# A graph network on one core: the sums of messages by destination are narrowed to 80 nodes, and the node stage's groups are put between them

## The chip, the cores and the metric

The kernel runs on one core of a Trainium2 chip. The metric is the device time of one execution in microseconds; the kernel before has a median of 4238.74 us over three runs (4227.38 to 4244.78). Engines are named as in the profile: PE is the matrix engine, PEld its loading of weights, DVE the vector engine, ACT the scalar engine, POOL the general engine (it also issues the indirect DMAs), SP the engine that only issues DMAs.

## What is computed

Two graph layers over 6250 nodes of 128 features and 100000 edges, each followed by a residual and a normalisation over the features. The edges come sorted by `dst`. The first layer is attention: a score for each edge and head, a softmax over the edges of one `src`, then the weighted values summed by `dst`. The second computes a message for each edge from both of its nodes and sums it by `src`.

```python
edge_index = jnp.stack([src, dst])
x = _layernorm(x + _L0_gnn_ref(x, edge_index, edge_attr_8, ...))
# first layer, cut:
weighted = v[src] * weights[:, :, None]
out = jax.ops.segment_sum(weighted, dest, num_segments=N).reshape(N, F)
return out @ Wo.T + bo
# second layer, cut:
edge_in = jnp.concatenate([x[row], x[col], edge_features], axis=-1)
h = jax.nn.silu(edge_in @ eW1 + eb1)
agg = jax.ops.segment_sum(jax.nn.silu(h @ eW2 + eb2), row, num_segments=N)
return jax.nn.silu(jnp.concatenate([x, agg], axis=-1) @ nW1 + nb1) @ nW2 + nb2
```

In the inputs, `dst` is the integer part of 6250 times the square of a uniform number. So edge number k of the sorted list has a `dst` near 6250 (k/100000)^2, and low nodes have many more edges than high ones.

## The kernel before

Edges are handled in tiles of 128, 784 tiles in all; 16 tiles are a chunk (49 chunks), 4 tiles a quad (196 quads). The first 9 chunks (region 0) go to the lowest nodes and are summed elsewhere, over the first 256 nodes. The rest, chunks 9 to 48, is region 1: 40 chunks, 160 quads. Nodes are handled in 49 blocks of 128.

The stages follow each other. A sort by `src` writes each edge's record to its place (up to line 898). The first layer's messages are computed in the order of `src` and scattered back to a table `xmsg` in the order of `dst` (L1008 and before). While the sort runs, `rows_of_keys` (L269) prepares what the later sums need: `d0q`, the first `dst` of each quad, and `dq`, each edge's `dst` less that of its quad. It also fills `bad`, a table of flags. If a flag is set (the keys don't have the form that the fast arm needs), `xflag` is 0 and a general arm runs in place of `fast()`. One of them (L322) is set where a `dst` lies 128 or more above its quad's first.

**Sums by dst** (L1090 to L1112). For each chunk one DMA loads its messages, `mt`, 1 MB, in turn from SP's and ACT's queue, with four buffers. For each quad DVE writes `ohd` (L1105), four one-hot matrices of 128 edges by 128 nodes, in one instruction of 512 elements a partition. PE multiplies (L1110): the messages of a tile are the stationary operand (128x128, f32), the one-hot matrix moves, and four products add up in one PSUM tile `ps` (six buffers). DVE adds `ps` to `agg` at the column of the quad's first node, which is read from a register (L1112). `agg` holds features by nodes.

**Node stage** (L1115 to L1170). The 49 blocks form 13 groups of four (the last has one). A group goes through three functions:

- `residual`: four products with `wo` into `po` (L1124), the bias added to `x_sb` by POOL (L1126; this depends on no sum, and all thirteen run early), `x_sb` plus `po` on DVE (L1127), and mean and variance per node on DVE (L902, L903).
- `normal`: the square root on ACT (L906), its reciprocal on DVE (L907), the normalisation in place, one DVE instruction per block (L1139), a transpose on PE (L1141) into `xp`, and a copy to `x1t` on ACT (L1142).
- `parts_of`: the products with `wab` into `pa` (L1151), halves copied by ACT (L1153) and added to `b1` by DVE (L1154), a store to `b_tab` from SP (L1156), a split of the other half into three bf16 parts by ACT and POOL in turn (L1161 to L1164), and a store to `a3_tab` (L1165; the profile names it a_tab).

```python
for g in range(len(groups) + 2):
    for lag, step in enumerate((residual, normal, parts_of)):
        if 0 <= g - lag < len(groups):
            step(g - lag)
```

**Edge stage** (from L1175). POOL gathers rows of `b_tab` (L118), SP loads one-hot rows (L1184), edge features (L1200) and windows of `a3_tab` (L1204), and PE works through 196 steps of four tiles.

Each engine takes its instructions in order. The order on an engine is not the one of the program's text: a scheduler in the framework places instructions by its own estimate of times, keeps dependencies, and adds the semaphores. Pools close at the end of a `with`, and their memory passes to the next.

## Time and profile before

| | us |
|---|---|
| three runs, median (lowest to highest) | 4238.74 (4227.38 to 4244.78) |
| the profiled execution | 4211.11 |
| its span | 4209.2 |
| from the last step before the sums to the last sum, about | 2954 to 3116 |
| node stage to the first gather of the edge stage | 3116 to 3174 |
| edge stage to the end | 3174 to 4209 |

Busy shares over the whole span: PE 63%, DVE 47%, ACT 20%, POOL 51%. The profile's page is one execution with every instruction's start and duration. Two kinds of answers are used besides the page. A timeline lists start, duration, engine, line, operation and tiles, with "x" and a number where equal instructions are merged. A table of windows gives, for a stretch, the busy time of each engine, the granted clock of PE as a share of full speed, and the DMA engines' share. An f32 product shows as two records on PE. Where a matmul's record overlaps the next one, the cost is read from start to start and not from its duration.

### The profile page before, as it was taken

Reading aid. Unit: us, or ns where it says so; the run is one execution under the profiler, and the core shown is the slowest. Engines: PE = TensorE matmul, PEld = TensorE weight load, DVE = VectorE, ACT = ScalarE, POOL = GpSimd, SP = SyncE. Lnnn points to the kernel's source line nnn. Section 1 sums busy time; section 2 is a strip of 40 time slices with the busy share of each in tenths; the row PEclk is TensorE's granted clock in tenths of the full one; section 3 lists DMA queues with packets and bytes.
Section 4 is the critical chain, followed back from the end, with each engine's and each line's share of the span. In section 5 each row is a group of like instructions: output and inputs, shape, how many; then the busy total and the mean of one; then the engine's idle time right before and its main releaser. Section 6 shows DMA issues by size and latency. Waiting matters only on the chain. (4 is left out here: it accounts for less than half of the span.)

```text
span 4209.2 us, 65902 instructions
## 1 busy us (share of the span) xinstructions
PE 2643.5 (63%) x22552; PEld 2030.1 (48%) x22552; DVE 1994.6 (47%) x6056; ACT 861.8 (20%) x2688; POOL 2156.6 (51%) x2119
## 2 busy tenths in 40 slices
PE   6546674444444225555655666565895999898988
PEld 4444443333333224444544555454883666665655
DVE  6655335454545525555555556554892222222232
ACT  2222232122222111111111111110022222222222
POOL 3455544555555551445445444556216666666663
PEclk8555555566555556666676777576897899999999
DMA  5433545444543315434434344431754333333341
GB/s 180 130 118 103 143 138 168 139 151 132 167 130 100 110 60 142 135 109 133 122 113 127 114 120 117 138 98 50 281 197 128 109 100 98 99 110 98 101 124 46
DMA packets 492378, 523.75 MB, mean 124 GB/s; under 512 B 155562, under 2 KB 417117, under 8 KB 486912
## 3 DMA queue, kind: packets, MB, share of 16 engines
q1 hardware_dynamic: 399150, 345.09, 28.3%
q0 software_dynamic: 66048, 140.62, 10.9%
q10 hardware_dynamic: 26834, 33.73, 2.5%
q8 instruction: 180, 2.95, 0.3%
q14 instruction: 166, 1.36, 0.1%
HBM read 391.11 MB, written 128.06 MB: 123 GB/s over the span
## 5 line engine op out<-in xcount | busy, mean ns | idle before, releaser
L126 POOL DMA_INDIRECT xs<-stg,posi x784 | 803.9, 1025 | 766.1 <-ACT cs L777 337.0
L126 POOL DMA_INDIRECT xmsg<-msg,at x640 | 648.7, 1014 | 722.1 <-issue 409.4
L118 POOL DMA_INDIRECT bt<-b_tab,dsti x640 | 640.5, 1001 | 333.4 <-issue 165.4
L778 PE MATMUL base<-hi,lo 128*128 128x49 bf16 x784 | 169.6, 216 | 547.3 <-ACT cs L777 333.5
L780 PEld LDWEIGHTS <-hit 128*128 128x128 bf16 x2352 | 145.7, 116 | 546.5 <-issue 531.0
L1259 DVE TENSOR_TENSOR stat_r<-stat_r,ps 128x128 f32 x232 | 66.3, 286 | 645.7 <-PE ps L1255 223.4
L787 PE MATMUL kx<-kw,ohd 128*128 128x128 bf16 x2352 | 265.5, 284 | 97.0 <-issue 56.9
L762 DVE TENSOR_SCALAR_CACHE_REDUCE junk<-sk,meta 128x127 bf16<-128x127 int16 x784 | 298.1, 435 | 11.4 <-DMA sk<-skew 4.8
L777 ACT CAST cs<-base 128x49 bf16<-128x49 f32 x784 | 160.7, 205 | 638.3 <-remote 286.4
L787 PEld LDWEIGHTS <-ohd 128*128 128x128 bf16 x2352 | 213.9, 131 | 136.1 <-issue 129.3
L587 PEld LDWEIGHTS <-oht 128*128 128x128 bf16 x2352 | 219.3, 134 | 124.3 <-issue 63.8
L1255 PE MATMUL ps<-ohf,fe 128*128 128x128 f32 x1568 | 231.4, 292 | 52.1 <-issue 28.5
L587 PE MATMUL qv<-qw,oht 128*128 128x128 bf16 x1920 | 200.5, 287 | 97.7 <-DVE oht L576 36.3
L1240 PE MATMUL po<-w_sb,ht 128*128 128x128 f32 x1568 | 245.6, 301 | 18.7 <-issue 9.4
L1255 PEld LDWEIGHTS ps<-ohf,fe 128*128 128x128 f32 x1568 | 208.8, 205 | 62.0 <-issue 33.9
L1240 PEld LDWEIGHTS po<-w_sb,ht 128*128 128x128 f32 x1568 | 205.2, 203 | 66.8 <-issue 49.4
L979 PE MATMUL qv<-vw,oht 128*128 128x128 bf16 x1920 | 188.5, 257 | 74.2 <-DVE pr L590 34.0
L1232 ACT ACTIVATE ht<-pre 128x512 f32<-128x512 f32 x196 | 116.9, 597 | 493.1 <-PE pre L1228 199.6
L979 PEld LDWEIGHTS <-oht 128*128 128x128 bf16 x1920 | 152.9, 117 | 122.6 <-issue 92.3
L223 DVE TENSOR_TENSOR lo<-iota_e,lo_c 128x2048 bf16<-128x2048 bf16 x98 | 119.0, 1215 | 150.6 <-remote 80.2
L780 PE MATMUL look<-st_b,hit 128*128 128x49 bf16 x1568 | 164.3, 211 | 27.1 <-DVE sel L794 17.0
L1228 PE MATMUL pre<-oht,aw 128*128 128x512 bf16 (+1 forms) x696 | 171.9, 365 | 12.8 <-issue 12.4
(303 smaller groups left out, 5228.8 us busy)
## 6 DMA issues: line engine op xcount, KB each, us to landing
st<-xs SPq DMA_DIRECT2D x49, 1128.0 KB
srow<-slo_row SPq DMA_DIRECT2D x98, 512.0 KB
lob<-lob_row SPq DMA_DIRECT2D x49, 512.0 KB
drow<-dlo_row SPq DMA_DIRECT2D x49, 512.0 KB
sk<-skew SPq DMA_DIRECT2D x49, 508.0 KB
qw<-q_tab SPq DMA_DIRECT2D x232, 96.0 KB
vw<-v_tab SPq DMA_DIRECT2D x232, 96.0 KB
aw<-a_tab SPq DMA_DIRECT2D x232, 96.0 KB
```

Of the source, the lines that this page charges most:

```text
L118: nc.gpsimd.indirect_dma_start(out=dst, out_offset=None, in_=table, in_offset=bass.IndirectOffsetOnAxis(ap=idx, axis=0))
L126: apart(nc.gpsimd.indirect_dma_start(out=table, out_offset=bass.IndirectOffsetOnAxis(ap=idx, axis=0), in_=src, in_offset=None), group)
L587: nc.tensor.matmul(qe[:, i, :], w["oh"][:, 4 * q + i, :], w["qw"][:, (4 * q + i) // WT[r], k, :], start=(k == 0), stop=(k == 2))
L762: nc.vector.tensor_scalar(junk, w["sk"][:, :, j], meta[:, c * UC + j, 0:1], 0.0, ALU.is_equal, ALU.add, accum_out=w["rank"][:, j:j + 1])
L777: nc.scalar.copy(cs, base)
L778: nc.tensor.matmul(base, lo, hi, start=False, stop=False, skip_group_check=True)
L780: nc.tensor.matmul(w["look"][:, j - 8 * h, :], w["hit"][:, j, :], tab, start=(i == 0), stop=(i == 2))
L787: nc.tensor.matmul(kx[:, i, :], w["ohd"][:, 4 * q + i, :], w["kw"][:, q, a, :], start=(a == 0), stop=(a == 2))
L979: nc.tensor.matmul(ve[:, i, :], w["oh"][:, 4 * q + i, :], w["vw"][:, (4 * q + i) // WT[r], k, :], start=(k == 0), stop=(k == 2))
L1228: nc.tensor.matmul(pre[:, i * wt:(i + 1) * wt, :], w["aw"][:, 4 // wt * q + i, k, :], w["oh"][:, 4 * q + i * wt:4 * q + (i + 1) * wt, :], ...
L1240: nc.tensor.matmul(po[:, i, :], ht[:, i, :], cw["w2"], start=False, stop=(i == 3))
L1255: nc.tensor.matmul(ps[:, i // WT[r], :], fe_[:, i, :], oh[:, i, :], start=(i % WT[r] == 0), stop=((i + 1) % WT[r] == 0))
```

## The change

There are four edits. The sums by `dst` use one-hot matrices, products and adds of 80 nodes (`WD`) instead of 128, and the flag is set at 80 in region 1. A second flag says that a quad's first `dst` must not lie over 64 nodes under the curve 0.16384 q^2 (q is the quad's number). By that curve `ready[g]` tells after which quad no later sum can reach the group g: 60, 82, 99, 114, 127, 139, 150, 160, 169, 178 and 187 for groups 0 to 10, of quads 36 to 195. The steps of these eleven groups are written between the quads, one step after a quad; groups 11 and 12 follow at the end, step by step. And the normalisation is done by ACT, as scale and bias of an ACTIVATE, with the bias `off`, minus mean times `rstd`, from DVE. `mt` gets five buffers instead of four, `ps` four instead of six, `po` and `xp` one instead of two; the zeroing of `agg2` and the load of `x_sb` are written one chunk earlier.

```diff
+WD = 80
+DST_SQ = 0.16384
+DST_SLACK = 64.0
...
-        nc.vector.tensor_single_scalar(b[:p, 1:2], b[:p, 1:2], float(P), ALU.is_ge)
+        nc.vector.tensor_single_scalar(b[:p, 1:2], b[:p, 1:2], float(WD if r else P), ALU.is_ge)
...
+            early = ks.tile([1, nt // 4], F32, name="early")
+            nc.gpsimd.iota(early, pattern=[[1, nt // 4]], base=t0 // 4, channel_multiplier=0,
+                           allow_small_or_imprecise_dtypes=True)
+            nc.vector.scalar_tensor_tensor(early, early, DST_SQ, early, ALU.mult, ALU.mult)
+            nc.vector.tensor_sub(early, early, d0qf)
+            nc.vector.tensor_reduce(b[0:1, 2:3], early, AX.X, ALU.max)
+            nc.vector.tensor_single_scalar(b[0:1, 2:3], b[0:1, 2:3], DST_SLACK, ALU.is_gt)
...
-        with tc.tile_pool(name="n0", bufs=3) as np_, tc.tile_pool(name="n0q", bufs=2, space=PSUM) as npq:
+        ready = [min(NQ, int((((j0 + n) * P + DST_SLACK) / DST_SQ) ** 0.5) + 1) for j0, n in groups]
+        with tc.tile_pool(name="fd", bufs=2) as dp, tc.tile_pool(name="fdp", bufs=4, space=PSUM) as dpp, \
+             tc.tile_pool(name="n0", bufs=3) as np_, tc.tile_pool(name="n0q", bufs=2, space=PSUM) as npq:
...
-                po = npq.tile([P, 4, F], F32, name="po")
+                po = npq.tile([P, 4, F], F32, name="po", bufs=1)
...
-                xp = npq.tile([P, 4, P], F32, name="xp")
+                off = np_.tile([P, 4, 1], F32, name="off")
+                nc.vector.scalar_tensor_tensor(off[:, :n], mv[:, :n, 0:1], -1.0, rstd[:, :n], ALU.mult, ALU.mult)
+                xp = npq.tile([P, 4, P], F32, name="xp", bufs=1)
                 for i in range(n):
-                    nc.vector.tensor_scalar(x_sb[:, j0 + i, :], x_sb[:, j0 + i, :], mv[:, i, 0:1], rstd[:, i, :],
-                                            ALU.subtract, ALU.mult)
+                    nc.scalar.activation(x_sb[:, j0 + i, :], x_sb[:, j0 + i, :], AF.Identity, bias=off[:, i, :],
+                                         scale=rstd[:, i, :])
...
+            def by_group():
+                for g in range(len(groups) - 2):
+                    for step in (residual, normal, parts_of):
+                        yield ready[g]
+                        step(g)
+                for step in (residual, normal, parts_of):
+                    for g in range(len(groups) - 2, len(groups)):
+                        yield NQ
+                        step(g)
+                yield NQ + 1
...
+            for c in range(AC, NC):
...
+                mt = dp.tile([P, UC, F], F32, name="mt", bufs=5)
...
+                if c == AC + 3:
+                    nc.gpsimd.memset(agg2, 0.0)
+                    nc.scalar.dma_start(x_sb, x_n)
+                for q in range(4):
+                    oh = dp.tile([P, 4, WD], F32, name="ohd", bufs=4)
...
+                    ps = dpp.tile([F, WD], F32, name="ps")
+                    for i in range(4):
+                        nc.tensor.matmul(ps, mt[:, 4 * q + i, :], oh[:, i, :], start=(i == 0), stop=(i == 3))
+                    to = agg[:, bass.ds(bs[4 * c + q - b0], WD)]
+                    nc.vector.tensor_add(to, to, ps)
+
+                    if due <= 4 * c + q + 1:
+                        due = next(node_steps)
+            while due <= NQ:
+                due = next(node_steps)
```

More of the change, by code (lines that the diff above doesn't have):

```diff
@@ L1089, in fast @@
         nc.scalar.copy(agg[:, :AB * P], nearby)
-        with tc.tile_pool(name="fd", bufs=2) as dp, tc.tile_pool(name="fdp", bufs=6, space=PSUM) as dpp:
-            pairs = xmsg.rearrange("(p t) f -> p t f", p=P)
-            for c in range(AC, NC):
-                if c == AC or c % 4 == 0:
-                    bs = regs(d0q, 4 * c, 4 * (4 - c % 4), ENG.DVE, NP - 1)
-                    b0 = 4 * c
-                mt = dp.tile([P, UC, F], F32, name="mt", bufs=4)
-                cuts = (0, 4, 8, 16) if c == AC else (0, 16)
-                for t0, t1 in zip(cuts, cuts[1:]):
-                    (nc.sync if c % 2 else nc.scalar).dma_start(mt[:, t0:t1], pairs[:, c * UC + t0:c * UC + t1, :])
-                if c == AC + 4:
-                    nc.gpsimd.memset(agg2, 0.0)
-                    nc.scalar.dma_start(x_sb, x_n)
-                for q in range(4):
-                    oh = dp.tile([P, 4, P], F32, name="ohd", bufs=4)
-                    nc.vector.tensor_tensor(
-                        oh, iota_f[:, None, :].to_broadcast([P, 4, P]),
-                        dq[:, c * UC + 4 * q:c * UC + 4 * q + 4, None].to_broadcast([P, 4, P]), ALU.is_equal)
-                    ps = dpp.tile([F, P], F32, name="ps")
-                    for i in range(4):
-                        nc.tensor.matmul(ps, mt[:, 4 * q + i, :], oh[:, i, :], start=(i == 0), stop=(i == 3))
-                    to = agg[:, bass.ds(bs[4 * c + q - b0], P)]
-                    nc.vector.tensor_add(to, to, ps)
         groups = [(j0, min(4, NB - j0)) for j0 in range(0, NB, 4)]
-        with tc.tile_pool(name="n0", bufs=3) as np_, tc.tile_pool(name="n0q", bufs=2, space=PSUM) as npq:
+        ready = [min(NQ, int((((j0 + n) * P + DST_SLACK) / DST_SQ) ** 0.5) + 1) for j0, n in groups]
+        with tc.tile_pool(name="fd", bufs=2) as dp, tc.tile_pool(name="fdp", bufs=4, space=PSUM) as dpp, \
+             tc.tile_pool(name="n0", bufs=3) as np_, tc.tile_pool(name="n0q", bufs=2, space=PSUM) as npq:
             held = {}
@@ L1165, in parts_of @@
                 nc.sync.dma_start(rows_of(a3_tab, j0, n), a3[:, :n].rearrange("p j i f -> p j (i f)"))
-            for g in range(len(groups) + 2):
-                for lag, step in enumerate((residual, normal, parts_of)):
-                    if 0 <= g - lag < len(groups):
-                        step(g - lag)
+            def by_group():
[8 more added lines that the diff above has]
+                yield NQ + 1
+            node_steps = by_group()
+            due = next(node_steps)
+            pairs = xmsg.rearrange("(p t) f -> p t f", p=P)
+            for c in range(AC, NC):
+                if c == AC or c % 4 == 0:
+                    bs = regs(d0q, 4 * c, 4 * (4 - c % 4), ENG.DVE, NP - 1)
+                    b0 = 4 * c
+                mt = dp.tile([P, UC, F], F32, name="mt", bufs=5)
+                cuts = (0, 4, 8, 16) if c == AC else (0, 16)
+                for t0, t1 in zip(cuts, cuts[1:]):
+                    (nc.sync if c % 2 else nc.scalar).dma_start(mt[:, t0:t1], pairs[:, c * UC + t0:c * UC + t1, :])
+                if c == AC + 3:
[3 more added lines that the diff above has]
+                    oh = dp.tile([P, 4, WD], F32, name="ohd", bufs=4)
+                    nc.vector.tensor_tensor(
+                        oh, iota_f[:, None, :WD].to_broadcast([P, 4, WD]),
+                        dq[:, c * UC + 4 * q:c * UC + 4 * q + 4, None].to_broadcast([P, 4, WD]), ALU.is_equal)
+                    ps = dpp.tile([F, WD], F32, name="ps")
[6 more added lines that the diff above has]
+            while due <= NQ:
+                due = next(node_steps)
         byd.close()
```

## The prediction

> **What bounds the kernel now.** The diff touches one stretch of the span, so I read it first in a table of three windows: the sums by dst, the node stage, the first 58 us of the edge stage. Columns: length, then busy us of PE, PE's weight loads, DVE, ACT, POOL, then granted clock, DMA share, GB/s.

> ```profile
> 2984.00:3116.00 132.00, 131.51 (x1176) 131.39 (x1176) 125.97 (x296) 0.00 (x0) 0.75 (x1) 1.00 0.79 270
> 3116.00:3174.00 58.00, 43.87 (x247) 35.14 (x246) 52.46 (x206) 33.72 (x79) 28.00 (x24) 0.99 0.41 131
> 3174.00:3232.00 58.00, 23.78 (x73) 12.33 (x73) 7.58 (x13) 4.70 (x8) 40.70 (x43) 0.56 0.43 125
> ```

> In the sums PE is never idle, DVE nearly never, ACT and POOL always. In the node stage DVE is busiest and PE still works 44 of 58 us. Next the timeline in the sums, to see who sets the pace:

> ```profile
> 3105.39 0.29 DVE L1112 TENSOR_TENSOR agg<-agg,ps 128x128 f32 x1
> 3105.59 0.68 DVE L1105 TENSOR_TENSOR ohd<-iota_f,dq 128x512 f32<-128x512 f32 x1
> 3106.28 0.29 DVE L1112 TENSOR_TENSOR agg<-agg,ps 128x128 f32 x1
> ```

> One quad per 0.89 us (3105.39 to 3106.28). The chain of waits has 131.60 us of PE ps L1110 x1176 in one piece: 0.1119 us a record, eight records a quad (four products, each two records), 0.895. Where DVE catches up (timeline, 2990.17 to 2990.97) a quad takes it 0.80. So **PE sets the pace, DVE is 10% behind it**.

> The node stage, from the chain (start, us, what):

> ```profile
> 3136.70 1.17 POOL res L1162
> 3137.89 0.63 ACT a L1163
> 3138.58 1.16 POOL a L1164
> 3139.74 0.69 issue
> 3140.47 1.17 POOL res L1162
> ```

> A period of 3.77 us per group: two POOL subtractions with casts on ACT between them. How it hands over, from SyncE's timeline:

> ```profile
> 3170.84 0.50 SPq L1156 DMA_DIRECT2D b_tab<-ab  x1
> 3173.80 7.41 SPq L1165 DMA_DIRECT2D a_tab<-a  x2
> 3182.64 0.34 SPq L1184 DMA_DIRECT2D srow<-slo_row  x1
> ```

> The last sum is added at 3116.40. b_tab's last store is issued at 3170.84 and POOL's first gather starts at 3174.06 (57.7 after the sum). The last a_tab store waits behind POOL's gathers, and SP reaches the edge stage's loads at 3182.64 (66.2 after). From there to 3232 PE waits for rows that SP loads.

> **Step 1, 80 columns instead of 128.** DVE: ohd is 0.683 us at 512 elements and the 256-element tensor_tensor of L113 0.411, so 1.06 ns an element; 192 fewer save 0.20, and 48 fewer in the add 0.05. DVE's quad goes from 0.80 to 0.55. PE is what counts: the moving side shrinks, the stationary side (mt, 128x128 f32, loaded anew for every record) doesn't. The trace has no f32 product at 80 columns. Low end: only columns count, 0.1119 x 80/128 = 0.070. High end: none do, 0.112. The nearest row is an f32 product with as large a stationary and 49 columns, at granted clock 0.50 (table of windows, 313 to 315), beside the sums' own product, also at 0.50 (2966 to 2968):

> ```profile
> 313.36 0.64 PE L356 MATMUL ps<-cnt,ones_f 128*128 128x49 f32 x2
> 313.80 0.63 PE L357 MATMUL ps<-cnt,after 128*128 128x49 f32 x2
> ```

> ```profile
> 2965.98 2.05 PE L1110 MATMUL ps<-ohd,mt 128*128 128x128 f32 x8 [6.91 <-DMA mt<-xmsg]
> ```

> Two records of 49 columns take 0.44 us from pair to pair, 0.22 each. The eight of 128: 2.05 less the last one's 0.55 is 1.50 over seven gaps, 0.214. So 49 columns cost as much as 128: **the weight load is the floor**, and at 128 columns the stream has just reached it. I take 0.1119 at 80 columns: step 1 gives PE nothing, and frees DVE.

> [...]

> **Step 2, eleven groups between the quads.** Per group of four blocks PE gets 8 records of po (0.112), 4 transposes (0.11) and 8 of pa with 256 columns (0.216; each from start to start of its line's records in the node stage, L1124, L1141, L1151): 0.90+0.44+1.73 = 3.06 us; eleven groups 33.7. PE is full, so all of it lengthens the sums. DVE per group: add 0.60, statistics 4x0.26, reciprocal and off 0.25, two adds of b1 0.66, together 2.6; 160x0.55 + 11x2.6 = 117 us, well under PE, so even POOL's hold on it is covered (with POOL's bias adds running before 2984, ohd took 1.55 instead of 0.68). ACT had 0.75 us there: free. DMA moved 270 GB/s at share 0.79 and 420 in 2966 to 2968; eleven groups' stores of 640 KB fit.

> New waits, by the changed kernel's order of instructions:
> - po reads agg, and the next dynamic add must wait for po. The order puts po 1.5 to 3 quads behind the add that it needs, so PE hardly waits for it; then the adds stand behind x_sb's add and the statistics on DVE, with four ps buffers now instead of six: about 0.3 us a group.
> - The transposes come 3.25 to 9.5 quads (2.9 to 8.5 us) after po. Their chain on DVE and ACT: 1.22 from po to the add (as at 3116.54 to 3117.76), add 0.60, sums and statistics 1.5, sqrt with its wait 0.5, reciprocal and off behind quads' work 1.0, first normalisation 0.6: 5.4. Groups 7 and 8 with 3.25 and 4 quads wait 1.7 and 1, four others 0.5, and a spacing of 0.40 on ACT against 0.2 to 0.45 on PE costs 0.2 a group: 7 us.
> - pa waits for x1t (0.58 and two handovers) behind 1.25 quads: 0.1 to 0.2 a group.

> Sum **11 us** (4 if every chain is hidden by the quads, 20 if ACT's and DVE's queues double it). mt's issues on ACT sit in front of square roots and copies, but each waits for a quad that PE passes before the transposes in question, so they cost nothing; with five buffers a load has 14 us.

> **Step 3, normalisation on ACT.** Four ACTIVATEs instead of four DVE instructions of 0.400. The nearest row with one pointer is L605 (0.405 at 129 elements); one without, L606, is 0.310. A second pointer: 0 to 0.1. ACT is free in the sums, so only the tail pays. What hides it otherwise is ACT's idleness; without that, 11x1.6 us.

> **Start.** x_sb still loads first, the first data still come at 2966. While POOL adds the bias (to 2984.7) ohd sets a pace of 1.68; five quads of that gain 0 to 3 us with the smaller ohd: 1.5.

> **The check** adds five DVE instructions and one POOL iota on 160 elements some 2.7 ms earlier: under 1 us, beside the sort's matmuls.

> **Step 4, the tail.** Only groups 11 and 12 (five blocks) follow. In us after PE's last work of the sums, each step by its row in the node stage of before (po as at 3116.54 to 3117.76, casts 0.62, POOL 1.16 and 0.43, ab 0.37): po and add 1.8, statistics 2.9, sqrt, reciprocal, off 3.7, five normalisations 5.9, transpose and x1t 7.2, ten records of pa 9.4, ab and b1's add 10.2, cast 10.9, res of both, cast, a of both 14.7. First gather at 15.2 (57.7 before), SP's loads at 16.5 (66.2 before, since POOL now ends a before it gathers). So 42.5 us by POOL, 49.7 by SP. I take SP's: PE's gaps from 3190 on end with what SP loads.

> **Sum.** The end of the sums moves by 33.7+11-1.5 = +43.2, from 3116.4 to 3159.6; the handover gives back 49.7: -6.5, or +0.7 by POOL. I take **-6**: 4211.1 (the profiled execution; its span is 4209.2) becomes 4205. The median of the runs shown, 4238.74, lies 0.66% above that execution, so the forecast for the median is **4233**. No change of under 0.5% (21 us) can be told from none here. PE's own work bounds the gain as well: with no stall at all the sums would end at 3148.6, 11 us earlier than I take, so step 1 as I price it allows 18 us at most.

> **Rivals.**
> 1. *Records shrink with the columns* (0.070). Quads then cost PE 0.57; DVE binds: 147x0.55 + 11x2.6 + 9 us of waits for po + 8 of POOL's hold from 2983 gives 3111, and the gain is 66.2-16.5+5 = 55: 4184. For it: bf16 products of 49 columns just beside L356 (L780, 314.23 to 314.46) come 0.04 apart, so few columns can be fast. Against: those in f32 aren't, and an f32 product's weight load shows 0.191 (L1151, L1124) where an f32 transpose's shows 0.141 (L1141). 13%, half-way records included.
> 2. *The node steps hold the quads* (slower). PE takes its instructions in order; if a transpose or pa not yet ready stops the quads behind it for more than the order planned, the stall is per group. With four ps buffers it can reach 3.5 to 4 us (5.4 of chain less what is queued ahead): 41 instead of 11, net +24: 4262. It decides from 3.5 us a group. Against: the order's 4 to 9 quads of distance, which at 0.89 last longer than at any faster pace. 15%.
> 3. *The wide arm isn't taken*: if a quad spanned 80 nodes the flag would choose the general arm. The reference's dst, sorted, spans at most 65 in a quad, and lies at most 21.3 nodes under the curve of the check, which allows 64. 1%, several hundred us slower, no estimate from this trace.

> **Numbers.** Forecast 71% (4233; by its own bounds, 4 to 20 us of stalls and 42 to 50 of handover, 4220 to 4250, and the runs' own spread of 17 us on top). Rival 1 13%, rival 2 15%, rival 3 1%. Range 4196 to 4263: it leaves out most of rival 1 and the far end of 2. Faster by over 0.5% (under 4217.5): rival 1 and a tenth of the forecast, 0.20. Slower (over 4260): two thirds of rival 2, rival 3 and some of the forecast, 0.15. Same 0.65.

> **What would show it.** Right: ps records with 80 columns still 0.11 apart at full clock; quads' stretches without groups 0.89 each; DVE with gaps in the sums; sums' end near 3160, first gather some 15 us later, SP's first edge load near 3176. Wrong: records near 0.07; PE idle over 2 us at every group; an edge stage that starts earlier than SP's loads allow or later than both.

## The result and the profile after

The changed kernel takes 4267.23 us (median of 8 runs, 4260.26 to 4285.08), the kernel before 4236.59 in the same comparison (8 runs, 4221.04 to 4245.91): **1.0085 times, 95% interval 1.0061 to 1.0109**, 31 us slower. The forecast was 4233, and 4267 lies above its range.

The profiled executions (4267.90 after, 4211.11 before) are 57 us apart, because the one of before was 25 us below its median. So I compare the stretch that the change touches. It is counted from the first record of DVE's one-hot line (a wait, at 2954.05 before and 2979.05 after; the first one-hot itself starts 0.78 us later in both). `fe` is the result of one step of the edge stage, written by ACT:

| us after that record | before | after | difference |
|---|---|---|---|
| last product of the sums ends | 162.0 | 226.5 | +64.5 |
| POOL's first gather of the edge stage | 220.0 | 250.1 | +30.1 |
| SP's first edge load | 228.6 | 249.3 | +20.8 |
| 12th `fe` on ACT (L1242 before, L1269 after) | 322.0 | 355.3 | +33.3 |
| end | 1255.1 | 1287.0 | +31.9 |

The last line, +31.9, is close to the difference of the medians, 30.6. The loss is in the sums; the hand-over gives half of it back.

The table of windows of after, for the start of the sums and a later stretch (length, then PE, its weight loads, DVE, ACT, POOL, granted clock, DMA share, GB/s):

```profile
2990.00:3040.00 50.00, 44.74 (x207) 44.37 (x208) 17.28 (x49) 0.00 (x0) 16.65 (x13) 0.50 0.58 217
3045.00:3105.00 60.00, 59.34 (x503) 57.93 (x501) 46.00 (x154) 15.09 (x34) 7.23 (x6) 1.00 0.82 276
```

The same for before:

```profile
2990.00:3040.00 50.00, 50.00 (x451) 50.00 (x450) 48.42 (x115) 0.00 (x0) 0.00 (x0) 1.00 0.87 296
```

In 50 us PE got through 207 records instead of 451. It waited for only 5 of the 50 us; it ran at **granted clock 0.50**, and DVE was busy a third of the time. The timeline of DVE in that stretch of after (start, us, instruction, and in brackets its wait and for whom):

```profile
3010.17 0.23 DVE L1192 TENSOR_TENSOR agg<-agg,ps 128x80 f32 x1
3011.47 0.49 DVE L1185 TENSOR_TENSOR ohd<-iota_f,dq 128x320 f32<-128x320 f32 x1 [1.07 <-PE ps L1190]
3011.88 0.23 DVE L1192 TENSOR_TENSOR agg<-agg,ps 128x80 f32 x1
```

A quad takes 1.71 us where it took 0.89, and DVE waits for PE in each. The timeline of PE shows when that ended:

```profile
3000.91 39.54 PE L1190 MATMUL ps<-ohd,mt 128*128 128x80 f32 x184 [1.46 <-DVE agg L1192]
3040.24 1.99 PE L1113 MATMUL po<-wo_sb,agg 128*128 128x128 f32 x8
```

184 records of 80 columns without a gap, 0.213 us each, and still half clock. It rose at 3044.1, 4 us after the first group's `po`, whose products have 128 columns. In before it rose 4.8 us after the stream of 128-column records had begun (at 2974.4; the stream at 2969.6). Of the steps from one record of the sums to the next, 249 lay at half clock in after and 37 in before (1242 of before's and 968 of after's at full clock; the others have a group's product in between). The hand-over at the end, on SP's queue:

```profile
3225.34 0.93 SPq L1156 DMA_DIRECT2D a_tab<-a  x2
3228.39 0.34 SPq L1211 DMA_DIRECT2D srow<-slo_row  x1
```

SP's first edge load now comes 22.8 us after the last product (3205.59), where the forecast had 16.5, and the first gather at 3229.14, 23.5 after it (15.2).

**Theory A**: an f32 stream of 80 columns doesn't raise the clock. **Theory B**, the rival: the gaps at the start, where `mt` is late, keep it low, whatever the columns. A second question is whether the stalls between quads (rival 2 of the prediction) cost anything beside that.

### The profile page after: what moved, and what is told of

Read it like the earlier page. It is cut to its first block, busy times and chain, and to the rows that moved or that the text cites. A ratio compares the mean times of both kernels' runs of the same rounds, so it can differ in the third digit from the quotient of the medians.

```text
span 4266.1 us, 65811 instructions
## 1 busy us (share of the span) xinstructions
PE 2654.5 (62%) x22552; PEld 2042.9 (48%) x22552; DVE 1945.7 (46%) x6024; ACT 886.9 (21%) x2737; POOL 2154.6 (51%) x2120
## 5 line engine op out<-in xcount | busy, mean ns | idle before, releaser
L990 PE MATMUL qv<-vw,oht 128*128 128x128 bf16 x1920 | 185.5, 255 | 72.4 <-DVE pr L601 33.7
L1190 PE MATMUL ps<-ohd,mt 128*128 128x80 f32 x1280 | 179.0, 303 | 19.5 <-DMA mt<-xmsg 12.8
L1190 PEld LDWEIGHTS ps<-ohd,mt 128*128 128x128 f32 x1280 | 176.2, 220 | 23.5 <-issue 13.9
```

Source lines behind the costliest of these rows:

```text
L990: nc.tensor.matmul(ve[:, i, :], w["oh"][:, 4 * q + i, :], w["vw"][:, (4 * q + i) // WT[r], k, :], start=(k == 0), stop=(k == 2))
L1190: nc.tensor.matmul(ps, mt[:, 4 * q + i, :], oh[:, i, :], start=(i == 0), stop=(i == 3))
```

## The experiments

The experiments ran on three chips, on which the kernel before takes 3254, 4299 and 4222 us; so each kernel is compared with the kernel before, or with its neighbours, on its own chip.

**The kernel before with 80 columns alone** (`e2`).

```diff
-                    oh = dp.tile([P, 4, P], F32, name="ohd", bufs=4)
+                    wd = 80
+                    oh = dp.tile([P, 4, wd], F32, name=f"ohd{wd}", bufs=4)
...
-                    to = agg[:, bass.ds(bs[4 * c + q - b0], P)]
+                    to = agg[:, bass.ds(bs[4 * c + q - b0], wd)]
```

> The kernel before with 80 columns in the sums and nothing else changed: node stage behind the sums, normalisation on DVE. No product of 128 or more columns stands in the sums that could raise the clock. Theory A: the whole sums run at half clock, 147 quads x 8 records x 0.10 us = 119 us more: 4340 to 4360. Theory B: the start is the one of the kernel before, where the clock rises 5 us after the stream begins, and the records cost 0.111 as with 128 columns: 4230 to 4240.

3381.42 us against 3253.76: 1.0400 (1.0382 to 1.0417), 128 us slower, a little more than theory A's 103 to 123; from its first product to its last the sums took 281.7 us, 158.8 in the next kernel. Windows and timeline of this kernel:

```profile
2250.00:2350.00 100.00, 100.00 (x470) 100.00 (x470) 37.61 (x117) 0.00 (x0) 0.00 (x0) 0.50 0.46 158
```

```profile
2194.75 266.23 PE L1111 MATMUL ps<-ohd,mt 128*128 128x80 f32 x1247
2461.40 6.08 PE L1125 MATMUL po<-wo_sb,agg 128*128 128x128 f32 x32 [0.42 <-DVE agg L1113]
```

PE was busy for all of 266 us and the clock stayed at 0.50; it rose at 2466.2, 4.8 us after `po` began. No group, no ACT, no new wait is in this kernel: theory A holds, theory B falls.

**Wide first, then narrow** (`e3`): 128 columns in the first five chunks. Against `e2`:

```diff
-                    wd = 80
+                    wd = P if c < AC + 5 else 80
```

> The kernel before with 128 columns in the first five chunks (20 quads, long enough for the clock to rise) and 80 in the other 35. It asks whether 80 columns only fail to raise the clock, or also lose it. Theory A, first form (a clock once granted is held by an unbroken stream of 80 columns): the records stay at 0.111, 4230 to 4245. Theory A, second form (80 columns don't hold it either): it falls some 5 to 20 us after the change of width, 140 quads x 8 x 0.10 = 112 us more: 4330 to 4350. Theory B: 4230 to 4240.

3252.14 against 3253.76: 1.0002 (0.9990 to 1.0014). The window after the change of width:

```profile
2250.00:2330.00 80.00, 80.00 (x717) 79.98 (x716) 57.41 (x183) 0.00 (x0) 0.00 (x0) 1.00 0.83 284
```

An unbroken stream of 80 columns **holds** the clock (1.00 to the end of the sums, some 130 us) that 266 us of it in `e2` didn't raise. At full clock a record costs what it cost with 128 columns (80.00 us over 717 are 0.112, and 0.1119 in before), so nothing is gained either.

**96 and 112 columns in the kernel before** (`b_before_96`, `b_before_112`), one execution each; the edit is that of `e2` with another number.

> The kernel before with 96 columns in all of the sums, to find how many columns raise the clock. 80 from the start left the whole sums at half clock. Theory (what counts is how much of a record's time the columns fill; a record lasts as long as 128 columns would, so 96 fill 0.75 of it and 80 fill 0.63): if the bound lies under 0.75 the clock rises within some 6 us of unbroken stream and the time is that of the kernel before; if it lies above, 1200 records cost 0.10 us more each, 119 us slower, as with 80. Rival (what counts is only whether PE is busy, and 80 columns failed for another reason, such as DVE's pace): the same 119 us with 96.

> The same with 112 columns (0.88 of a record). If 96 raise the clock this does too, and the time is that of the kernel before within its spread. If 96 don't: between the time of the kernel before and 119 us more, by where the bound lies.

4233.88 and 4234.07, inside the kernel before's runs on that chip (4199.35 to 4243.59, median 4221.53). With 96 the clock rose 5.0 us after the stream began (at 2997.3; the stream at 2992.3), with 112 5.1 us after, and with 96 the next stretch is that of 128 columns:

```profile
2992.31 11.69 PE L1111 MATMUL ps<-ohd,mt 128*128 128x96 f32 x80 [1.66 <-DMA mt<-xmsg]
```

```profile
3000.00:3050.00 50.00, 49.18 (x437) 48.76 (x436) 41.92 (x109) 0.00 (x0) 6.21 (x5) 1.00 0.83 279
```

With 80 columns from the start the clock stayed at 0.50 until the first `po` on two other chips (`e2`, `a0`); no run has a width between 80 and 96, and each clock is that of one execution. What the clock goes by, columns per record or something that goes with them, no run shows.

**The changed kernel with 128 columns** (`e1`).

```diff
-WD = 80
+WD = 128
```

> The changed kernel with one constant back: quads sum over 128 columns instead of 80; groups between the quads and normalisation on ACT stay. In the profile of the changed kernel 249 of the sums' records run at granted clock 0.5 (37 before), most of them in one unbroken stretch of 39 us at the start, and the clock rises only when the first group's 128-column products come. Theory A (an f32 stream of 80 columns counts as too little work to raise the clock): with 128 columns the clock is full within some 6 us of unbroken stream; 200 fewer records at half clock, 200 x 0.10 = 20 us less, less 1 to 3 for DVE's wider one-hots while POOL adds the bias: 4245 to 4250. Theory B (the gaps at the start, where mt is late, keep the clock low, whatever the columns): the half-clock stretch stays until the first group, 4262 to 4272.

1.0069 (1.0050 to 1.0088) of the kernel before, 16 to 29 us slower, where 8 to 13 would have met the expectation. The clock did rise 5.8 us after the stream began (43 records at half clock). The sums lasted 210.8 us from their first product to their last, against 219.0 in the changed kernel. The interval reaches into theory B's 25 to 35, so the time doesn't tell the two apart; the clock, which rose before the first group, decides for A. What was missing went into DVE, which needs 0.80 us a quad again. PE's waits behind the start (line, waited for: us in total, times, longest):

```profile
PE ps L1190 <- DVE ohd L1185: 6.2, 12, 0.7
PE ps L1190 <- DVE agg L1192: 3.6, 3, 1.6
PE po L1113 <- DVE agg L1192: 3.5, 3, 2.6
PE xp L1132 <- ACT x_sb L1130: 1.8, 3, 1.1
```

So the groups between the quads gain from the narrow one-hots, on DVE: with 128 columns in the first 20 quads alone (`a1` below) the sums take 8.7 us less.

**Changed kernel as it is, with 128 columns first, with DVE's normalisation, with the pools in another order** (`a0` to `a3`, one chip, 4299.06 us for the kernel before).

> The changed kernel as it is, as the reference of the other three on the same chip: 30 us (20 to 40) slower than the kernel before, in the sums (half clock at the start) and the hand-over to the edge stage.

4337.54 (1.0075, 1.0035 to 1.0115). First product to last: 220.8 us; first gather 248.9 us after the first record of DVE's one-hot line.

```diff
-                    oh = dp.tile([P, 4, WD], F32, name="ohd", bufs=4)
+                    wd = P if c < AC + 5 else WD
+                    oh = dp.tile([P, 4 * P], F32, name="ohd", bufs=4)[:, :4 * wd].rearrange("p (t e) -> p t e", t=4)
```

> The changed kernel with 128 columns in the first five chunks (20 quads) and 80 in the other 35; all else as changed. In the kernel before, 80 columns from the sixth chunk on held the clock. Theory A (the clock isn't raised by 80 columns, but is held by them): it rises within some 6 us of unbroken stream, some 200 records cost 0.11 instead of 0.21; less 2 to 4 us because DVE writes 512 elements a quad while POOL adds the bias: 15 to 22 us faster than the changed kernel as it is. Theory B (what was lost lies in the stalls between the quads, and a full clock at the start only brings the next wait forward): 0 to 6 us faster.

4314.77 (1.0047, 1.0022 to 1.0072): 23 us less than `a0` by the medians, 12 by the ratios, whose intervals overlap. The profiles decide: the sums lasted 202.1 us, 18.7 less than in `a0` (43.2 more than before's 158.9), and the first gather comes 15.6 us earlier (233.3). PE's waits in them, without those for the first loads:

```profile
PE ps L1191 <- DVE ohd L1186: 3.3, 6, 0.8
PE ps L1191 <- DVE agg L1193: 2.8, 2, 2.0
PE xp L1132 <- ACT x_sb L1130: 0.7, 1, 0.7
```

6.8 us over eleven groups, 0.6 a group. The stalls are there and small; the clock was the larger loss.

```diff
-                    nc.scalar.activation(x_sb[:, j0 + i, :], x_sb[:, j0 + i, :], AF.Identity, bias=off[:, i, :],
-                                         scale=rstd[:, i, :])
+                    nc.vector.tensor_scalar(x_sb[:, j0 + i, :], x_sb[:, j0 + i, :], mv[:, i, 0:1], rstd[:, i, :],
+                                            ALU.subtract, ALU.mult)
```

> The changed kernel with the normalisation back on DVE (four instructions of 0.40 us a group instead of four ACTIVATEs and the one for off); groups stay between the quads, 80 columns stay. Theory (ACT was idle in the sums, and at 80 columns DVE has room, so it matters little which of them normalises): within 5 us of the changed kernel as it is. Rival (DVE's queue is what stops PE: each group's four instructions stand in front of the adds, 11 x 1.5 us): 10 to 18 us slower than the changed kernel.

4338.74 (1.0087, 1.0054 to 1.0121), 1 us from `a0` by the medians (its sums lasted 223.6 us, 220.8 there): who normalises mattered little here (in after ACT was busy for 15 of the 60 us from 3045, DVE for 46).

```diff
-        with tc.tile_pool(name="fd", bufs=2) as dp, tc.tile_pool(name="fdp", bufs=4, space=PSUM) as dpp, \
-             tc.tile_pool(name="n0", bufs=3) as np_, tc.tile_pool(name="n0q", bufs=2, space=PSUM) as npq:
+        with tc.tile_pool(name="n0", bufs=3) as np_, tc.tile_pool(name="n0q", bufs=2, space=PSUM) as npq, \
+             tc.tile_pool(name="fd", bufs=2) as dp, tc.tile_pool(name="fdp", bufs=4, space=PSUM) as dpp:
```

> The changed kernel with the node stage's pools opened ahead of the sums' pools instead of behind them, so that their memory is where it was in the kernel before; nothing else. In the changed kernel's profile the first gather starts 3.4 us after POOL's last subtraction, together with SP's first edge load and DVE's first edge instruction, just when the last store to a_tab has landed. Theory (the gather's buffers took over memory of the node stage's pools and so waited for that store): the first gather starts 0.3 to 1 us after the last subtraction, 2 to 4 us faster than the changed kernel as it is. Rival (the gather waits for b_tab's store or for code, wherever its buffers lie): no change, within 2 us.

The hand-over on POOL, in the changed kernel:

```profile
3224.16 1.54 POOL L1155 TENSOR_TENSOR a<-res,a 128x512 bf16<-128x512 f32 x2 [0.34 <-ACT a L1154]
3229.14 0.99 POOL L121 DMA_INDIRECT bt<-b_tab,dsti  x1 [3.44 <-issue]
```

and in this one:

```profile
3288.80 1.54 POOL L1155 TENSOR_TENSOR a<-res,a 128x512 bf16<-128x512 f32 x2 [0.34 <-ACT a L1154]
3290.49 0.99 POOL L121 DMA_INDIRECT bt<-b_tab,dsti  x1 [0.15 <-issue]
```

3.44 us became 0.15, as the theory said: the gather's buffers had taken over memory of the node stage, and waited for its last store. On the whole time (4329.89 against 4337.54; 1.0065, 1.0035 to 1.0095) the runs are too far apart to say more.

**Normalisation on ACT alone, in the kernel before** (`e4`).

```diff
+                off = np_.tile([P, 4, 1], F32, name="off")
+                nc.vector.scalar_tensor_tensor(off[:, :n], mv[:, :n, 0:1], -1.0, rstd[:, :n], ALU.mult, ALU.mult)
...
-                    nc.vector.tensor_scalar(x_sb[:, j0 + i, :], x_sb[:, j0 + i, :], mv[:, i, 0:1], rstd[:, i, :],
-                                            ALU.subtract, ALU.mult)
+                    nc.scalar.activation(x_sb[:, j0 + i, :], x_sb[:, j0 + i, :], AF.Identity, bias=off[:, i, :],
+                                         scale=rstd[:, i, :])
```

> The kernel before with the normalisation on ACT (four ACTIVATEs and one more DVE instruction a group) and nothing else. The node stage has a period of 3.77 us a group, set by POOL's subtractions and ACT's casts. ACT's work per group becomes 0.59 + 2x0.37 + 2x0.62 + 0.29 + 4x0.40 = 4.5 us. Theory (ACT then binds the node stage): 13 x 0.7 = 9 us more, 4242 to 4250. Rival (DVE, busiest engine of that stage, is what set its start-up and its end, and gains 1.5 us a group): 2 to 8 us less, 4229 to 4235.

1.0037 (1.0023 to 1.0051), 7 to 17 us slower, as the theory said. From the last product of the sums to the first gather are 71.8 us instead of 58.0. From one group's first subtraction on POOL to the next group's the first five periods take 4.0 to 5.0 us instead of 3.77 (2372.52, 2377.48 and 2382.06 for three of the starts), and from 2363 to 2381 ACT is busy 15.74 of 18 us: ACT binds there. Two later periods take 9.2 and 7.5 us; between 2380 and 2405 the granted clock fell to 0.50 three times, so not all of the loss is shown to be ACT's own work.

**Both mends, and a group more at the end** (`a4`, `a5`).

> The changed kernel with both mends: 128 columns in the first five chunks, and the node stage's pools opened ahead of the sums' pools. The first alone left it 1.0047 times the kernel before and moved the first gather 15.6 us forward, the second alone moved the first gather 3.4 us closer to the last sum. Theory (the two add up, since the one is PE's pace in the sums and the other a store's landing behind them): 5 to 13 us slower than the kernel before. Rival (the first gather's time doesn't set the end, since the start-up of the edge stage waits for SP's loads): 12 to 18 us slower, as with the first mend alone.

```diff
-                for g in range(len(groups) - 2):
+                for g in range(len(groups) - 3):
...
-                    for g in range(len(groups) - 2, len(groups)):
+                    for g in range(len(groups) - 3, len(groups)):
```

> As the kernel with both mends, and only ten groups between the quads; three follow at the end. In the changed kernel the last two sums on DVE stood 3.3 us behind group 10's additions of b1, which wait for pa. Theory (that place is worth 3 us, a group between the quads costs 3.06 us of PE and 0.5 of stalls, a group at the end costs one more period of POOL, 3.8): 2 to 4 us faster than with both mends alone, 2 to 10 us slower than the kernel before. Rival (the end costs more per group than the place between the quads): 0 to 4 us slower than with both mends alone.

`a4`: 4243.53 against 4221.53, 1.0041 (1.0017 to 1.0065). The gains add up at the first gather, 230.1 us against 248.9 in `a0` and 220.0 in the kernel before (218.8 and 219.6 with 96 and 112 columns on this chip). The medians are 22 us apart, above both expectations; the ratio says 17 us, in the rival's range, and its interval (7 to 27) covers much of both. That the first gather counts can't be read from the time. `a5`: 4241.57, 1.0052 (1.0030 to 1.0074). Its last sum was added 0.3 us after the last product, not 3.5, but from there to the first gather took 21.5 us instead of 16.7. Its first gather is 0.5 us earlier (229.6), between theory and rival, and the times can't tell them apart. No version of the interleaving beats the kernel before.

## Why the prediction was wrong, by its steps

**Step 1, 80 columns. Here it failed.** The price at full clock was right: 878 of the 968 full-clock steps of after are 0.111 or 0.112 us, DVE's one-hots take 0.485 us. "Step 1 gives PE nothing" was not: it assumed the granted clock of before. 212 more steps at half clock x 0.102 = 21.6 us, and the groups' own products that ran at half clock (8 records of `pa` x 0.21, 8 of `po` and 4 transposes x 0.10) 2.9: 24.5 us that the prediction's sum had at nothing. Before had no long stream of narrow f32 products, so its trace couldn't show this; the row at 49 columns that I leaned on was itself at clock 0.50, and I read only its spacing.

In the runs that begin with 96, 112 or 128 columns the clock rose 3.5 to 5.8 us after their stream began (4.8 in before, 5.0 with 96, 5.1 with 112, 5.8 in `e1`). In the run with 80 columns (`e2`) it didn't: 266 us of unbroken products at half clock. That the weight load sets the price at full clock was my estimate from the rows at 49 and 128 columns. The runs show the price alone: 0.111 to 0.112 us with 80 columns, 0.111 with 96 (719 records in the 80 us from 3050) and 0.1119 with 128.

**Step 2, eleven groups.** The 33.7 us of PE's own work were right (32.0 of them ahead of the last product of the sums; group 10's `pa` comes behind it). The stalls were too high: 11 forecast, 6.5 in after (4.7 for adds, 1.8 for one-hots), of which before has 1.7. PE's waits in the sums of after, then of before:

```profile
PE ps L1190 <- DMA mt<-xmsg: 12.8, 3, 7.6
PE ps L1190 <- DVE agg L1192: 4.7, 4, 2.0
PE ps L1190 <- DVE ohd L1185: 1.8, 3, 1.1
```

```profile
PE ps L1110 <- DMA mt<-xmsg: 11.7, 3, 6.9
PE ps L1110 <- DVE ohd L1105: 1.7, 4, 0.5
```

The sum, 32.0 + 24.5 + 6.5 - 1.7, and 1.1 more of waits for `mt`, is 62.4; the first table has 64.5, and the other 2 us aren't placed. In `a1`, without most of the clock's share, the sums lasted 43.2 us longer than before; that this is the forecast's number is chance, since its terms differ. One stall cost twice: PE waited 2.0 us for an add, and the clock was at half from 3149.9 to 3160.1.

```profile
3147.51 3.98 PE L1190 MATMUL ps<-ohd,mt 128*128 128x80 f32 x24 [2.04 <-DVE agg L1192]
```

The same wait stands in `a0`, `a1`, `a3`, `a4` and `a5`, and in each of them 6.8 to 10.2 us at half clock follow; in `a2` three pauses of 1.15 to 1.34 us are followed by 3.4 us each, while behind one of 1.06 us in after the clock stayed full. With 128 columns (`e1`) it stayed full over pauses of up to 1.2 us.

**Start.** Instead of 1.5 us less, it took 1.1 us more of waits for `mt`. The first data came at 2957.2 in before, not at 2966, and the first product in after 7.5 us after the first `mt` was issued (3.1 before). `x_sb`'s load, 3.1 MB, is issued 0.01 us after that `mt`, not 0.29. The other profiles go with this order: 7.6 to 8.6 us in `a1`, `a2` and `a4` (at most 0.01 us apart), 3.0 to 3.5 in `a0`, `a3`, `e1` and the kernels with 96 and 112 columns (0.13 to 0.29 apart). No run changed the order alone, so the cause is argued.

**Step 3, ACT.** Right in the sums (`a2`), and only there (`e4`).

**Step 4, the tail.** In us after the last product (3205.59):

| | forecast | after |
|---|---|---|
| `po` and add | 1.8 | 5.5 |
| statistics | 2.9 | 6.9 |
| normalisations | 5.9 | 10.2 |
| `pa` | 9.4 | 15.8 |
| last `a` | 14.7 | 20.1 |
| first gather | 15.2 | 23.5 |

First, the last sums on DVE stood behind group 10's additions of b1. From DVE's timeline:

```profile
3205.49 0.23 DVE L1192 TENSOR_TENSOR agg<-agg,ps 128x80 f32 x1
3207.04 0.42 DVE L1145 TENSOR_TENSOR ab<-pa,b_sb 128x256 f32<-128x256 f32 x1 [1.32 <-issue]
3207.80 0.42 DVE L1145 TENSOR_TENSOR ab<-pa,b_sb 128x256 f32<-128x256 f32 x1 [0.34 <-ACT ab L1144]
3208.14 0.23 DVE L1192 TENSOR_TENSOR agg<-agg,ps 128x80 f32 x1
3208.29 0.68 DVE L1296 TENSOR_TENSOR x_sb<-x_sb,nb_sb 128x512 f32<-128x512 f32 x1
3208.89 0.23 DVE L1192 TENSOR_TENSOR agg<-agg,ps 128x80 f32 x1
```

That is 3.7 us in the first row. PE waited 1.9 us for the last add, the granted clock fell to 0.50 at 3211.3, and `pa`'s ten records, still at 0.50, took 4.5 us, 2 more than forecast. Last, the store's landing, 3 us (`a3`). And "I take SP's": the gain was POOL's. From the first gather to the 12th `fe` are 102.0 us in before, where SP's first load comes 8.6 us after the gather, and 103.3 to 105.9 in after and `a0` to `a3`, where it comes 0.8 us ahead to 2.6 behind (to the 20th `fe` 145.4, and 142.5 to 148.8). So the 7.2 by which SP's 49.7 exceeds POOL's 42.5 were never there. Misses of 21.3 (sums), 8.3 (tail) and 7.2 make 36.8 of the 38.4 us between -6.5 and +31.9.

**Rivals.** Rival 1 was wrong. Rival 2's time, 4262, came near, but by chance, since its mechanism was wrong: 0.6 us a group, not 3.5. Of "what would show it", the records' spacing at full clock and DVE's gaps came as forecast, and of the signs of being wrong the late edge stage came.

Open: `a4` loses 5.9 us from the first record of the one-hot line to the end in its profile, 17 by the ratio and 22 by the medians; what the rest is wasn't found.

## What to carry to other kernels

Here an f32 product with 80 columns behind a weight load of 128 gained nothing on PE (0.112 us a record at full clock, as with 128) and, from the start, lost half of the clock (0.50 over 266 us in `e2`); after any narrowing read the granted clock first, and if it must be narrow, begin wide (`e3`: 1.00) and leave no pauses (behind those of 2.0 us came 6.8 to 10.2 us at half clock). Work put between the instructions of the engine that set the pace wasn't hidden here: 33.7 us of PE's work moved into a stage without idle PE, to shorten one in which PE was idle for only 14 of 58 us. At a hand-over, look whose memory the next stage takes (`a3`: 0.15 us of wait instead of 3.44), and count from the instruction that starts it, not from the one that ends last.
